# A list scheduler for a transformer kernel, with plain exponentials and the norms' small steps on GpSimd

## The chip, the core and the metric

The kernel runs on one core of one Trainium2 chip. The metric is the device time of one execution in microseconds. Lower is better. The engines are called PE (TensorE, matrix products and transposes), DVE (VectorE), ACT (ScalarE, activations and copies), POOL (GpSimd) and SP (SyncE, which issues most DMAs). All of them run at the same time, each through its own queue in a fixed order, and wait for one another through semaphores. SBUF is the on-chip memory; PSUM has eight banks of 128 x 512 floats, into which PE writes.

## What is computed

The input x has 32 batch elements of 128 tokens and 128 channels. A cross attention with 16 heads and a time bias comes first, then six layers of local attention and feed forward. In short:

```python
x = x + xattn(layernorm(x), ctx, ctx, deltas, mask)      # 16 heads, 4 key groups, head size 8
h = layernorm(x)
y = h
for i in range(6):
    y = attn(shift_tokens(y), Wqkv[i], q_scale[i], k_scale[i], Wo[i]) + y
    y = ffn(shift_tokens(y), ln_g[i], ln_b[i], W1[i], b1[i], W2[i], b2[i]) + y
x = x + y

def shift_tokens(t):     # second half of the channels comes from the token before
    a, s = split(t, 2, -1);  return concat([a, pad(s, one token)[:-1]], -1)

def attn(x, Wqkv, qs, ks, Wo):          # 16 heads of 64
    q, k, v = split(x @ Wqkv)
    q = rotary(l2norm(q) * qs);  k = rotary(l2norm(k) * ks)
    # windows of 32 tokens; each token sees the 32 tokens before it and itself
    return softmax(mask(8 * q @ k.T)) @ v @ Wo

def ffn(x, g, b, W1, b1, W2, b2):       # 341 hidden channels
    a, gate = split((layernorm(x) * g + b) @ W1 + b1)
    return (a * gelu(gate)) @ W2 + b2
```

## The kernel before

**Tiling.** A *unit* is one batch element in one layer: 128 tokens on the partitions. There are 6 x 32 = 192 units. Four batch elements form a *group* (GB = 4); each layer has eight groups, and the feed forward works on a whole group at once, 48 times in all. Matrix products with full precision are made of three products of parts (`split3`, lines 636 to 638).

**A unit.** PE makes four tiles of 128 x 512 queries and keys (`qk`, names pqk). ACT squares each (line 686), DVE sums the squares of each head (line 689) and multiplies the tile with two tables for the rotary embedding (line 694, two products t of 512 columns for each tile), POOL adds the two (line 700, result rt). Then comes the inverse norm of all 32 heads, `rsqrt_a`, `rsqrt_b`, `rsqrt_c`: a floor on DVE (line 118), a logarithm and an exponential on ACT (lines 126 and 128), and one Newton step in three small operations on DVE (lines 133, 135, 137). POOL multiplies the four rt tiles with it (line 723), PE transposes them (line 729), ACT copies the queries out (line 735) and the halves of the keys (lines 739 and 746; one half per unit goes to DVE, line 744). The values go through the output projection at once (`y`, names py), ACT copies them (line 762), and sixteen small DMAs on SP's queue lay each unit's rows out by windows (line 769, tiles ysh). The scores of half the heads lie in one PSUM bank (lines 781 and 786). DVE takes the row maxima (line 793). ACT makes the exponentials, eight pieces of 64 columns for each half, and each piece adds up its sum in an accumulator that a further instruction reads out (line 804). DVE inverts the sums (line 809), POOL scales the weights (line 813), DVE transposes them (line 817), and PE multiplies them with ysh (line 830, pO).

**A group.** Its input is transposed and shifted on PE: for each of the four elements, one transpose of half the channels and one product with a shift matrix for the others (lines 660 and 661, ax), written as two parts by ACT and DVE. After the four units come the residual (line 848), a DMA that shifts half of the channels by one token (line 851), the layer norm with the same `rsqrt` steps on 4 columns (line 116 and the shared lines), PE's products, three gelus on ACT (line 910) and the second product (line 935). After the third gelu, line 912 asks for one particular table of ACT's functions by name:

```python
            if i == 2:
                nc.scalar.preload_act_table_set("natural_log_exp_and_others")
```

The same call stands once in the prologue (line 140). ACT keeps one table of functions at a time; where an instruction needs a function that the table at hand lacks, the compiler puts a load (ACT_TABLE_LOAD) ahead of it.

**Order.** The order is written out by hand. `OFF`, `GOFF`, `OFF1` and `GOFF1` hold one place on a common scale for every operation of a unit, a group and the cross attention; `push` puts each operation into a heap by its time (a unit is given T = 13.3, a group four times that), and `drain` issues them in that order. Each engine's queue follows it. Buffers come from pools that rotate: five PSUM banks for products (pj), two for scores, one for the attention's result; eight rt, four yt, three kb.

**Weights.** The next layer's weights are loaded and split while the present layer runs (`prep_ops`), with places in the same scale.

Of the kernel before, what the change touches and what calls it, by code (L numbers as in the profile page):

```python
# [8 lines left out]
F32 = mybir.dt.float32  # L9
# [7 lines left out]
P = 128  # L17
# [5 lines left out]
NRT = 8  # L23
NYT = 4
NKB = 3
NQT = 3
EWD = (1,)
STORE = 0.4
MP1 = [23.0 + 1.2 * i for i in range(8)]
WV1, DH1, DL1 = [20.85, 22.05], 0.15, 0.3  # L30
PREP0, PREPT = 10.0, 7.0
SHIFT = 6.0
FFT = 7.0
MP = [31.47, 31.72, 31.97, 32.22, 32.47, 32.72, 32.97, 33.22]
WV, BIAS, DH, DL = [24.4, 25.4], 16.4, 0.06, 0.14
T1 = 7.0
NI1 = 180
OFF1 = dict(
    sc=[[0, 2, 26, 28], [32, 34, 73, 75], [93, 95, 139, 141], [154, 159, 170, 172]],
    mx=[[1, 3, 27, 29], [33, 35, 74, 76], [94, 96, 140, 142], [158, 164, 171, 173]],  # L40
    sb=[[4, 5, 30, 31], [36, 37, 77, 78], [97, 98, 143, 144], [165, 168, 174, 175]],
    ex=[[39, 41, 44, 48], [99, 100, 101, 102], [151, 152, 155, 160], [187, 189, 192, 196]],
    tp=[[42, 46, 51, 55], [126, 127, 128, 129], [153, 157, 163, 167], [190, 194, 199, 203]],
    st=[[45, 50, 54, 57], [130, 132, 134, 135], [156, 162, 178, 179], [193, 198, 202, 205]],
    pa=[[49, 53, 82, 83], [131, 133, 136, 137], [161, 166, 186, 188], [197, 201, 218, 220]],
    oT=[[84], [138], [191], [223]], pb=[[145], [146], [195], [227]], rl=[[147], [148], [200], [232]],
    at=[[149], [150], [204], [236]],
)
GOFF1 = dict(
    ldc=[-101], gst=[-121, -120], gr0=[-119], gr1=[-117, -116], gr2=[-115, -114, -113], xa=[-118], xb=[-112],  # L50
    px=[-89], pxe=[-88], pcx=[-100], pce=[-99], pk=[-77], ke=[-76], kd=[-75], pq=[-74, -73, -71, -67],
    qe=[-72, -69, -65, -62], qd=[-70, -66, -63, -60], pv=[-55], vt=[-11], td=[-110], ab=[-109, -108], ln=[-4],
    mkb=[-56], tbm=[-3], p2=[238], aT=[249], pw=[265], rs=[266], hst=[267, 268], hr0=[269], hr1=[292, 296],
    hr2=[299, 301, 302], xf1=[270], xf2=[303],
)
T = 13.3
NI = 331
OFF = dict(
# [28 lines left out]
def body(ctx: ExitStack, tc: tile.TileContext, x, ctx_in, fside, mask, xWq, xWk, xWv, xWo, xtw,  # L87
         Wqkv, q_scale, k_scale, Wo, ln_g, ln_b, W1, b1, W2, b2, cst, x1d, out):
    nc = tc.nc
    B = x.shape[0]  # L90
    L = Wqkv.shape[0]
    HID = W2.shape[1]
    NG = B // GB
    HC = [(0, 128), (128, 128), (256, HID - 256)]
    RT = HC[2][1]

# [939 lines left out]
```

## Time and profile before

| | us |
|---|---|
| median of 3 runs | 3326.27 |
| lowest and highest | 3325.03, 3327.11 |
| span of the profiled execution, first to last instruction | 3320.9 |
| PE busy in that span | 3155.8 |
| DVE busy | 2979.5 |
| ACT busy | 2834.9 |
| POOL busy | 2468.3 |
| 48 table loads ahead of a gelu (L910), 48 after (L912) | 61.6 each |

The profiled execution's own time is given only as its span. Busy time counts instructions at work; register, semaphore and DMA-issuing instructions are left out. In a row of instruction groups one reads the line of the source, the engine, the operation, the tile written and the tiles read with their shapes, how often, then busy time in us and the mean of one in ns, and last the engine's idle time just before them with what ended it. Instructions of one engine can overlap at their ends, so busy time divided by the count can be less than the mean of one.

### The profile page before, as it was taken

What the parts mean: (1) busy time and instruction counts of PE and PEld (TensorE: products, weight loads), DVE (VectorE), ACT (ScalarE), POOL (GpSimd) and SP (SyncE); (2) the same over time, 40 slices, a digit from 0 to 9 for tenths busy, and PEclk for the clock granted to TensorE, in tenths of its full rate; (3) what the DMA queues carried; (4) which work ended last, traced back from release to release, by engine and by line L of the source; (5) the groups of instructions that cost most, each with busy time, mean ns of one, the idle gap of its engine ahead of it and who ended that gap; (6) DMA issues with size and microseconds to landing.
All of it is one profiled execution on the core that took longest, in us unless ns stands there. A gap on an engine that the chain in (4) does not pass through costs nothing.

```text
span 3320.9 us, 102077 instructions
## 1 busy us (share of the span) xinstructions
PE 3155.8 (95%) x35979; PEld 2389.3 (72%) x35979; DVE 2979.5 (90%) x6954; ACT 2834.9 (85%) x9983; POOL 2468.3 (74%) x2284
## 2 busy tenths in 40 slices
PE   8999899999999999999999999999999999999997
PEld 5555677777777777777777777777777777777775
DVE  6666899999999999999999998998999998999995
ACT  6776888898888898889898889898888898898895
POOL 5655777777787777787787787786787776777873
PEclk9999999999999999999999999999999999999998
DMA  2110333332333332233332333332333332333332
GB/s 61 33 37 12 77 87 82 79 74 71 75 83 86 78 74 72 72 85 84 77 77 71 75 83 81 79 77 68 79 83 76 84 76 64 77 82 81 82 83 62
DMA packets 217966, 243.80 MB, mean 73 GB/s; under 512 B 83534, under 2 KB 112498, under 8 KB 217458
## 3 DMA queue, kind: packets, MB, share of 16 engines
q1 hardware_dynamic: 217026, 236.93, 28.8%
q8 instruction: 288, 4.72, 0.6%
q14 instruction: 220, 1.80, 0.2%
q10 hardware_dynamic: 432, 0.34, 0.0%
HBM read 25.31 MB, written 4.19 MB: 9 GB/s over the span
## 4 chain that ended last, share of the span: by engine, by line
PE 49%; DVE 32%; ACT 8%; issue 4%; DMA 3%; SPq 2%; POOL 1%; ACTq 0%; DVEq 0%; POOLq 0%
DVE t L694 10%; PE pO L830 8%; PE ptq L729 7%; DVE ss L689 6%; PE sc L786 4%; DVE rnv L118 3%; PE pa L542 3%; PE pqk L636 3%; PE pqk L638 3%; ACT pr L804 3%; PE pqk L637 3%; DVE mx L793 2%; DVE PT L817 2%; SPq L769 2%; PE py L636 2%
## 5 line engine op out<-in xcount | busy, mean ns | idle before, releaser
L700 POOL TENSOR_TENSOR rt<-t,t 128x512 f32<-128x512 f32 x768 | 980.3, 1286 | 372.8 <-DVE t L694 330.8
L694 DVE TENSOR_TENSOR t<-pqk,tab 128x512 f32<-128x512 f32 x1536 | 983.3, 681 | 115.9 <-ACT sq L686 110.3
L804 ACT ACTIVATE pr<-sc,mx 128x64 f32<-128x64 f32 x3072 | 915.7, 331 | 61.2 <-DVE PT L817 53.0
L723 POOL TENSOR_TENSOR rt<-rt,rny 128x512 f32<-128x512 f32 x768 | 777.4, 1043 | 214.1 <-DVE rny L137 213.4
L804 ACT ACTIVATION_READ_ACCUMULATOR pr<-sc,mx 128x1 f32 x3072 | 691.9, 225 | 0.0
L689 DVE TENSOR_REDUCE ss<-sq 128x8 f32<-128x512 f32 x768 | 517.4, 674 | 0.0
L830 PE MATMUL pO<-ysh,PT 128*32 128x128 f32 x10752 | 416.9, 275 | 53.3 <-DVE PT L817 48.7
L813 POOL TENSOR_TENSOR pr<-pr,rl 128x512 f32<-128x512 f32 x384 | 400.8, 1044 | 89.2 <-DVE rl L809 89.2
L686 ACT ACTIVATE sq<-pqk 128x512 f32<-128x512 f32 x768 | 429.3, 600 | 24.6 <-PE pqk L638 12.5
L830 PEld LDWEIGHTS pO<-ysh,PT 128*32 128x32 f32 x10752 | 367.1, 110 | 97.6 <-DVE PT L817 72.1
L762 ACT COPY yt<-py 128x512 f32<-128x512 f32 x768 | 416.8, 614 | 21.2 <-PE py L638 17.2
L729 PE MATMUL ptq<-cs,rt 128*128 128x128 f32 x3072 | 409.8, 278 | 22.2 <-DVE t L694 17.0
L729 PEld LDWEIGHTS ptq<-cs,rt 128*128 128x128 f32 x3072 | 334.5, 141 | 96.7 <-issue 52.5
L786 PE MATMUL sc<-kb,qT 128*32 128x128 f32 (+1 forms) x12288 | 375.1, 262 | 15.2 <-DVE kb L744 14.8
L786 PEld LDWEIGHTS sc<-kb,qT 128*32 128x32 f32 x12288 | 270.7, 109 | 114.5 <-issue 70.7
L636 PE MATMUL py<-mw,xsh 128*128 128x512 f32 x768 | 333.1, 434 | 8.9 <-ACT yt L762 5.8
L636 PE MATMUL pqk<-wqh,xsh 128*128 128x512 f32 x768 | 314.0, 409 | 4.8 <-ACT yt L762 2.8
L638 PE MATMUL py<-mw,xsl 128*128 128x512 f32 x768 | 301.9, 393 | 0.0
L638 PE MATMUL pqk<-wqh,xsl 128*128 128x512 f32 x768 | 300.9, 392 | 0.0
L637 PE MATMUL pqk<-wql,xsh 128*128 128x512 f32 x768 | 300.8, 392 | 0.0
L637 PE MATMUL py<-mw,xsh 128*128 128x512 f32 x768 | 300.6, 391 | 0.0
L735 ACT COPY qT<-ptq 128x512 f32<-128x512 f32 x384 | 208.1, 590 | 79.0 <-PE ptq L729 78.1
(168 smaller groups left out, 5756.8 us busy)
## 6 DMA issues: line engine op xcount, KB each, us to landing
ysh<-yt SPq DMA_DIRECT2D x3072, 64.0 KB
raw<-in_L_ffn_Wqkv SPq DMA_DIRECT2D x36, 256.0 KB
xsu<-xt SPq DMA_DIRECT2D x48, 127.0 KB
wor<-in_L_ffn_Wo SPq DMA_DIRECT2D x6, 512.0 KB
xt<-in_x SPq DMA_DIRECT2D x8, 256.0 KB
cx<-in_ctx SPq DMA_DIRECT2D x8, 256.0 KB
mk<-in_mask_BxS_ff SPq DMA_DIRECT2D x8, 256.0 KB
x_scratch<-xt SPq DMA_DIRECT2D x8, 256.0 KB
```

What stands on the lines that cost most here:

```text
L636: nc.tensor.matmul(pt, lh, rh, start=True, stop=False)
L637: nc.tensor.matmul(pt, lh, rl, start=False, stop=False)
L638: nc.tensor.matmul(pt, ll, rh, start=False, stop=True)
L686: nc.scalar.activation(V["sq", c], V["pp", c], AF.Square)
L689: nc.vector.tensor_reduce(V["ss"][:, c * 8:(c + 1) * 8], V["sq", c].rearrange("p (h d) -> p h d", d=64), axis=AX.X, op=ALU.add)
L694: nc.vector.tensor_tensor(V["t", k, c].rearrange("p h s d -> p h (s d)"), V["pp", c].rearrange("p (h d) -> p h d", d=64), w["tab"][:, c // ...
L700: nc.gpsimd.tensor_tensor(V["rt", c], V["t", 0, c], V["t", 1, c][:, :, ::-1, :], op=ALU.add)
L723: nc.gpsimd.tensor_tensor(rv, rv, V["rn"][:, c * 8:(c + 1) * 8].unsqueeze(2).to_broadcast([P, 8, 64]), op=ALU.mult)
L729: nc.tensor.transpose(V["ptq", c][:, k, :], V["rt", c][:, 2 * k:2 * k + 2].rearrange("p h s d -> p (h s d)"), ident)
L786: nc.tensor.matmul(sc[32 * c:32 * c + 32, :, wd, lo:64], qT[:, c, 32 * wd:32 * wd + 32], kT[:, c, :, 32 * wd - 32 + lo:32 * wd + 32], star ...
L804: nc.scalar.activation(pr[:, q, :], scv[:, q, :], AF.Exp, bias=mx[:, q:q + 1], accum_out=ls[:, q:q + 1])
L830: nc.tensor.matmul(pO[32 * wd:32 * wd + 32, j, :], PT[:, half, wd, blk, :], ysh[u][:, (2 * par + half) * P:(2 * par + half + 1) * P], star ...
```

## The change

The whole emission is rewritten. An operation is now recorded with its engine, two costs, a priority, and the buffers that it reads and writes (`S.op`). `Sched.run` then plays the engines in time: an engine that is free takes the first ready operation by priority (the unit's number plus a shift by name, `LATER`) whose buffers are to be had, and the order in which operations start is the order of issue. Costs are in a table by name (`COST`, an engine, the time that it is held, and the time to the result). Operations marked "E" or "G" need ACT's exponentials or gelus: a switch between the two adds 1.3 to the held time, and after a switch to "G" nothing marked "E" starts until three gelus have. Buffers are handed out by the scheduler: six PSUM banks for products, one for scores, one for the attention's result; ten rt, three yt, two kb, two t of 1024 columns.

In the operations themselves:

- The exponentials are eight plain activations for each half; one DVE operation adds up all eight sums (`sm`).
- The two table products of a tile are one DVE operation of 1024 columns (`tab`).
- The floor and the Newton step of every norm are five small operations on POOL (`newton`); logarithm and exponential stay on ACT.
- Both halves of the keys are copied by ACT (`evk`).
- A group's input tile has 192 columns: the channels, with the shifted half behind them. The shift is two DMAs, after the residual and after the feed forward (`shift`), and the shift products on PE are gone (`ax` is four transposes).
- The call that names ACT's table stands in the prologue only.

```diff
-        def tk(k, c):
-            V["t", k, c] = wk2.tile([P, 8, 2, 32], F32, tag=f"t{k}", name=f"t{k}")
-            nc.vector.tensor_tensor(V["t", k, c].rearrange("p h s d -> p h (s d)"),
-                                    V["pp", c].rearrange("p (h d) -> p h d", d=64),
-                                    w["tab"][:, c // 2, k, :].unsqueeze(1).to_broadcast([P, 8, 64]), op=ALU.mult)
+            S.op("tab", lambda: nc.vector.tensor_tensor(
+                t.t.rearrange("p (k h d) -> p k h d", k=2, d=64),
+                pp.t.rearrange("p (h d) -> p h d", d=64).unsqueeze(1).to_broadcast([P, 2, 8, 64]),
+                tab.t[:, c // 2].unsqueeze(2).to_broadcast([P, 2, 8, 64]), op=ALU.mult), pri, [pp, tab], [t])
...
-                nc.scalar.activation(pr[:, q, :], scv[:, q, :], AF.Exp, bias=mx[:, q:q + 1],
-                                     accum_out=ls[:, q:q + 1])
+                def ex(i):
+                    for k in range(4 * i, 4 * i + 4):
+                        nc.scalar.activation(pr.t[:, k * 64:(k + 1) * 64], sc.t[:, k * 64:(k + 1) * 64], AF.Exp,
+                                             bias=mx.t[:, k:k + 1])
+                for i in range(2):
+                    S.op("ex", lambda i=i: ex(i), pri, [sc, mx], [pr], table="E")
+                S.op("sm", lambda: nc.vector.tensor_reduce(sm.t, r8(pr), axis=AX.X, op=ALU.add), pri, [pr], [sm])
...
-        if eps is not None:
-            nc.vector.tensor_scalar(v, src, eps, None, op0=ALU.add)
-        else:
-            nc.vector.tensor_scalar(v, src, floor, None, op0=ALU.max)
...
-        if c == 0:
-            nc.vector.tensor_tensor(t, y, y, op=ALU.mult)
-        elif c == 1:
-            nc.vector.scalar_tensor_tensor(t, v, -0.5, t, op0=ALU.mult, op1=ALU.mult)
-        else:
-            nc.vector.scalar_tensor_tensor(y, t, 1.5, y, op0=ALU.add, op1=ALU.mult)
...
+    def newton(names, pri, V, src, n, floor, eps, pool_, cols):
+        v, y, t = [Buf(p) for p in pool_]
...
+        def f0():
+            if eps is not None:
+                nc.gpsimd.tensor_scalar(sl(v), cols(), eps, None, op0=ALU.add)
+            else:
+                nc.gpsimd.tensor_scalar(sl(v), cols(), floor, None, op0=ALU.max)
+
+        def f1():
+            nc.scalar.activation(sl(y), sl(v), AF.Ln)
+
+        def f2():
+            nc.scalar.activation(sl(y), sl(y), AF.Exp, scale=-0.5)
+
+        def f3():
+            nc.gpsimd.tensor_tensor(sl(t), sl(y), sl(y), op=ALU.mult)
+
+        def f4():
+            nc.gpsimd.tensor_tensor(sl(t), sl(t), sl(v), op=ALU.mult)
+
+        def f5():
+            nc.gpsimd.tensor_scalar(sl(t), sl(t), -0.5, 1.5, op0=ALU.mult, op1=ALU.add)
+
+        def f6():
+            nc.gpsimd.tensor_tensor(sl(y), sl(y), sl(t), op=ALU.mult)
+        S.op(names[0], f0, pri, [src], [v])
+        S.op(names[1], f1, pri, [v], [y], table="E")
+        S.op(names[2], f2, pri, [y], [y], table="E")
...
-            if i == 2:
-                nc.scalar.preload_act_table_set("natural_log_exp_and_others")
...
-                nc.tensor.transpose(G["ptx"][0:64, k, :], xb[:, 0:64], ident)
-                nc.tensor.matmul(G["ptx"][64:128, k, :], xb[:, 64:128], shift, start=True, stop=True)
...
+            nc.sync.dma_start(xt[g][1:113, :, 128:192], xt[g][0:112, :, 0:64])
+            nc.sync.dma_start(xt[g][113:P, :, 128:192], xt[g][112:P - 1, :, 0:64])
+        S.op("psh", f, pri, [X[g]], [XS[g]])
...
+                for o in cand[e]:
+                    if o.ready > t + 1e-9:
+                        continue
+                    if o.table and o.table != table and hold:
+                        continue
...
+                occ = o.occ
+                if o.table and o.table != table:
+                    table = o.table
+                    occ += 1.3
+                    if table == "G":
+                        hold = 3
+                if o.table == "G":
+                    hold -= 1
```

## The prediction

> **What bounds the kernel now.** I read the engines' shares first, then one steady stretch, then the instructions of that stretch.
>
> The page's first part and the head of its chain:
>
> ```profile
> PE 3155.8 (95%) x35979; PEld 2389.3 (72%) x35979; DVE 2979.5 (90%) x6954; ACT 2834.9 (85%) x9983; POOL 2468.3 (74%) x2284
> ...
> PE 49%; DVE 32%; ACT 8%; issue 4%; DMA 3%; SPq 2%; POOL 1%; ACTq 0%; DVEq 0%; POOLq 0%
> ```
>
> PE sets the end and DVE is close behind; ACT has only 15% to give. Busy time by stretch (columns: length, then PE, PEld, DVE, ACT, POOL, the granted clock, DMA share, GB/s):
>
> ```profile
> 200.00:300.00 100.00, 95.58 (x609) 56.30 (x609) 65.89 (x436) 68.50 (x141) 54.01 (x52) 1.00 0.05 14
> ...
> 1000.00:2000.00 1000.00, 964.16 (x11528) 747.19 (x11518) 935.22 (x1884) 885.28 (x3229) 771.98 (x709) 1.00 0.32 78
> ```
>
> The granted clock is full, so the work itself is the limit. The second stretch is inside the six layers. ACT's groups there give the unit of account:
>
> ```profile
> L804 ACT ACTIVATE pr<-sc,mx 128x64 f32<-128x64 f32 x1038 | 309.4, 331 | 19.7 <-DVE PT L817 17.1
> L804 ACT ACTIVATION_READ_ACCUMULATOR pr<-sc,mx 128x1 f32 x1038 | 233.9, 225 | 0.0
> L686 ACT ACTIVATE sq<-pqk 128x512 f32<-128x512 f32 x260 | 145.1, 600 | 6.3 <-PE pqk L638 2.5
> ...
> L746 ACT COPY kb<-ptq 64x512 f32<-64x512 f32 x65 | 37.8, 582 | 0.8
> L910 ACT ACT_TABLE_LOAD x16 | 20.5, 1283 | 0.3
> L912 ACT ACT_TABLE_LOAD x16 | 20.5, 1283 | 0.3
> ```
>
> A unit (one batch element in one layer) squares four times, so 260 squares are 65 units: one unit lasts 1000/65 = 15.38 us. Per unit PE is busy 964.16/65 = 14.83, DVE 14.39, ACT 13.62, POOL 11.88. There are 6 x 32 = 192 units, so 1 us per unit is 192 us of the kernel. Every change below is judged by which of these four becomes the largest.
>
> **The change, part by part, per unit.**
>
> **Exponentials (ACT).** All work on the tile pr took ACT 321.30 us in the stretch, for 1038/8 = 129.75 halves: 2.48 us a half. Without accumulators 8 plain pieces stay. None of 64 columns stands alone in this trace. The nearest row is four neighbours of 128 columns, also with a bias column per partition:
>
> ```profile
> 102.10 1.14 ACT L485 ACTIVATE kb<-pd,nct 128x128 f32<-128x128 f32 x4
> ```
>
> One lasts 0.373 (its group's mean), so the other three start (1.14 - 0.373)/3 = 0.256 apart. A 512-column copy starts about 0.49 after the one before it; from there to 0.256 is 0.234 for 384 columns, 0.61 ns a column, so 64 columns fewer is about 0.04 to 0.05: 0.21 a piece. Bounds: 0.13 (a 128x4 activation without a bias column starts so soon after another) and 0.256. At 0.21 a half is 7 x 0.21 + 0.33 = 1.80; the unit saves 2 x 0.68 = 1.36. With the bounds it saves 2.5 or 0.7.
>
> **Key copies (ACT, DVE).** One half copy per unit goes from DVE (L744, 0.695) to ACT, where its twin L746 takes 0.582: ACT +0.55, DVE -0.70.
>
> **Table loads (ACT).** This is the part that the diff hardly shows. The old line 912 loads the combined table by hand after each gelu; the new kernel has no such line outside the prologue. In the instruction order of the built program ACT then holds 534 table loads, against 97 before: 1 at the start, 48 ahead of a gelu, 230 ahead of a logarithm and 255 ahead of an exponential. The logarithm's loads name another table than the exponential's, so each norm flips twice. The logarithm and exponential of a norm stand one copy or square apart, with a load ahead of each. All 437 extra loads lie behind the first gelu: 437/192 = 2.28 per unit. The scheduler's table rule knows just two states, gelu and not gelu, so its order has no room for them. What one costs:
>
> ```profile
> 459.36 1.28 ACT L910 ACT_TABLE_LOAD   x1
> 460.65 1.83 ACT L910 ACTIVATE u<-pg,b1c 128x512 f32<-128x512 f32 x3
> 462.50 1.28 ACT L912 ACT_TABLE_LOAD   x1
> 463.80 1.08 ACT L735 COPY qT<-ptq 128x512 f32<-128x512 f32 x2
> ```
>
> From the gelus' end (462.48) to the next copy (463.80) is 1.32, and the overlap of about 0.1 that neighbours have (two copies in 1.08, 0.59 alone) is lost: 1.42. Bounds 1.28 and 1.42; I take 1.42: 2.28 x 1.42 = 3.24 us of ACT per unit. A load does not wait with the logarithm behind it, so it could use idle time of ACT; but the sum below leaves ACT none.
>
> Here the Trainium skill has a rule, and a harsher price. The page "ScalarE: Activation LUTs", section "Table sets: the hidden batching unit", says that one set holds both exp and ln and that mixing sets costs a load at each switch: the old order obeys, the new one does not. Its section "What ACT_TABLE_LOAD costs" gives 1283 ns plus a drain of 1380, 2.66 us a switch. The trace shows the 1283 to the digit, and 1.32 in all from end to start, no drain. By the rule the unit would pay 2.28 x 2.66 = 6.06, by the rows 3.24. I use the rows; the rule is a rival.
>
> ACT in sum: 13.62 - 1.36 + 0.55 + 3.24 = 16.05 us, above the present unit of 15.38.
>
> **Norm steps (DVE to POOL).** DVE loses 0.853 + 0.490 + 0.244 + 0.192 = 1.78 per unit for the queries' and keys' norm (L118, L133, L135, L137), and (0.733 + 0.212 + 0.925 + 0.417)/4 = 0.57 for the feed forward's. POOL gets five small operations for each. No such small one is in the trace. The line through
>
> ```profile
> L880 POOL TENSOR_TENSOR xn<-xn,fry 128x512 f32<-128x512 f32 x16 | 16.6, 1041 | 0.2
> ...
> L868 POOL TENSOR_TENSOR xn<-xsu,fmv 128x256 f32<-128x256 f32 x16 | 9.8, 616 | 0.0
> ```
>
> has 1.66 ns a column and 0.19 fixed: 0.24 for 32 columns, 0.20 for 4 (an estimate; bounds 0.12, the small clears of this trace, and 0.49, what DVE's L133 takes). POOL +5 x 0.24 + 5 x 0.20/4 = +1.45, to about 13.3. The first of the last four steps waits for the exponential; behind it in POOL's queue stand the multiplications by the norm and the additions that free the two t buffers, on which DVE's table products wait, and they hold PE's banks. In the new order POOL has a mean of 3.05 us of other work between its first step and that wait, but under 2.5 us in 88 of 192 units. The trip through ACT is two loads, two short activations and a copy: 2 x 1.42 + 2 x 0.27 + 0.5 = 3.9. So POOL stalls some 1.2 us per unit even if ACT comes at once: 14.5. That is below ACT's 16.05, but it passes ACT's lateness on.
>
> **Sums, table products (DVE).** Two sums a unit, one for each half, as L689 (0.674): +1.3. One 1024-wide product replaces two 512-wide ones: two take 1.28, so 0 to 0.15 each is saved; I take 0.08 x 4 = 0.3. DVE: 14.39 - 1.78 - 0.57 - 0.70 + 1.3 - 0.3 = 12.3.
>
> **Group input (PE).** Twelve narrow transposes and shift products go; from 1653.44 to 1655.79 they held PE for 2.35 us. Four plain transposes replace them, which start 0.42 before the next work (1643.39 to 1643.81): -1.9 per group, -0.48 per unit. PE: 14.35.
>
> **At nothing.** The shift now comes by DMA: 192 small DMAs instead of 48 on SP's queue. For the feed forward it was a DMA before; for the next layer's input there are seven other groups (seven times 61 us) to hide it. Behind a waiting shift stand the ysh transfers, which free the yt buffers (three instead of four); SP now waits 825.9 us in all for yt, so its queue has room. If that cover went, ACT's copies would wait; 0 to 0.2 us per unit. One score bank instead of two and two kb instead of three tie PE closer to ACT: a half's loop (scores 1.2, maximum 0.65, exponentials 1.8, hand-overs) is about 4 of every 8 us, hidden. The cross attention's work stays, and its norms come before the first gelu.
>
> **The sum.** Per unit: ACT 16.05, PE 14.35, POOL 13.3 with stalls 14.5, DVE 12.3. ACT becomes the bound. PE as the bound reached 14.83/15.38 = 96.4% busy. ACT's order was made without these loads, but the other engines have more slack than before, so I take 96%: 16.05/0.96 = 16.72. The unit grows by 1.34, 192 units by 257 us. The page gives the profiled execution as its span, 3320.9; the median of the runs is 5.4 above it, which I leave as it is: 3326.3 + 257 = 3583.
>
> **The rivals.**
>
> POOL's wait rules (20%): if ACT reaches the logarithm late by one burst of exponentials (1.8), the trip is 5.7 and POOL stalls about 2.7, to 16.0; two rings of equal length that wait for each other would run at perhaps 17.5: +2.1 x 192 = +400, 3730. For it: the queue's order. Against it: POOL's slack and ten rt buffers.
>
> The drain is real (4%): 18.9/0.96 = 19.7, +820, 4150. Against it: the rows above.
>
> Loads fall into idle time (10%): ACT pays 1.28 and the pieces cost less, 0.17: 13.62 - 1.9 + 0.55 + 2.92 = 15.2, at 97.5% 15.6: 3370 to 3450.
>
> Faster (4%): the exponentials' piece decides. At 0.13 it saves 2.5 and ACT, with loads of 1.28, needs 14.6; at 97.5% the unit is 15.0: -70, about 3255. The gain begins below 0.15 a piece, where ACT falls under 15.0. Against it: the row of 0.256, and the accumulator read itself starts 0.2 behind its piece.
>
> **How the numbers follow.** Likeliest (62%): 3583; between ACT 97.5% busy and 93% it gives 3533 to 3690. The range 3430 to 3760 leaves about 1 in 10 on each side: the last two rivals and the low edge of idle-time loads below, the drain and the upper part of POOL's case above. A difference under 0.2% (7 us) couldn't be told from none. Faster 0.04 is the last rival; same 0.02 lies between it and the idle-time loads; slower 0.94 is the rest.
>
> **What would show it.** In the changed profile: table loads of 1283 ns, 534 in number and some 685 us in sum; ACT the busiest engine in the layers, at 95% or more; PE near 86% of a unit of 16.7; POOL's wait for the exponential among the largest; the exponential's piece near 0.21 apart; DVE under 80%. It is wrong if ACT's busy share stays below 90% (then a wait rules), or if the loads overlap other ACT work.

## The result

The changed kernel takes 3763.83 us (median of four runs, 3758.95 to 3772.6) against 3325.65 for the kernel before: 1.1321 times as long, with a 95% interval of 1.1305 to 1.1337. That is 438 us more; 257 were forecast, and the time lies 4 us above the forecast's range. The profiled execution's span is 3757.1.

The first part of the page, and the stretches of the trace that answer to those shown of before (length; then PE, PEld, DVE, ACT, POOL busy; granted clock, DMA share, GB/s):

```profile
PE 3368.1 (90%) x35595; PEld 2335.1 (62%) x35595; DVE 2616.4 (70%) x5156; ACT 3225.6 (86%) x7540; POOL 2734.6 (73%) x3528
```

```profile
200.00:300.00 100.00, 91.42 (x529) 54.06 (x529) 55.95 (x367) 63.95 (x122) 49.44 (x60) 0.98 0.07 18
...
1000.00:2000.00 1000.00, 895.37 (x10009) 630.53 (x10008) 714.64 (x1146) 897.77 (x2112) 748.71 (x963) 0.97 0.30 69
```

No engine is full any more. In the layers PE and ACT are both at 90%, and the granted clock is 0.97 where it was 1.00. The unit of account is read most exactly from the residuals, 48 of four units each (the row gives, after the count, the shortest, median and longest of them in ns, and the start of the first and the last). First before, then after:

```profile
L848 DVE TENSOR_TENSOR xt<-pO,xt x48: 635/640/692, 402.2 to 3287.6; 128x512 f32<-128x512 f32 x48
```

```profile
L840 DVE TENSOR_TENSOR xt<-bank__68,xt x48: 674/680/692, 449.7 to 3729.9; 128x512 f32<-128x512 f32 x48
```

Between the first and the last lie 47 groups, 188 units: (3287.6 - 402.2)/188 = 15.35 us before and (3729.9 - 449.7)/188 = 17.45 after. The layers grow by 2.10 x 188 = 395 us, the head up to the first residual by 47, and the end is 6 shorter: 436 between the two spans. Busy time per unit is now PE 15.62, ACT 15.67, DVE 12.47, POOL 13.07 (the second stretch's numbers times 17.45/1000).

The table loads, in the groups of the page:

```profile
L374 ACT ACT_TABLE_LOAD x230 | 295.1, 1283 | 4.1
L377 ACT ACT_TABLE_LOAD x221 | 283.5, 1283 | 3.9
...
L873 ACT ACT_TABLE_LOAD x48 | 61.6, 1283 | 0.8
L812 ACT ACT_TABLE_LOAD x34 | 43.6, 1283 | 0.6
```

With the one at the start that is 534, and 685 us. ACT's queue around one norm, in the timeline (start, length):

```profile
1088.15 1.75 ACT L812 ACTIVATE pr__13818<-bank__67,mx__13883 128x64 f32<-128x64 f32 x8
...
1089.71 0.60 ACT L768 COPY kb__82<-bank__63 64x512 f32<-64x512 f32 x1
1090.33 0.58 ACT L769 COPY kb__82<-bank__63 64x512 f32<-64x512 f32 x1
1090.92 1.28 ACT L374 ACT_TABLE_LOAD   x1
1092.22 0.23 ACT L374 ACTIVATE ry__13953<-rv__13923 128x32 f32<-128x32 f32 x1
1092.47 0.59 ACT L765 COPY qT__13886<-bank__64 128x512 f32<-128x512 f32 x1
1093.08 1.28 ACT L377 ACT_TABLE_LOAD   x1
1094.37 0.23 ACT L377 ACTIVATE ry__13953<-ry__13953 128x32 f32<-128x32 f32 x1
```

Each load holds ACT for 1.30, from its start to that of the next instruction; the rows show no drain behind it. The eight exponentials of a half take 1.75.

### The profile page after: what moved, and what is told of

It reads as the page before. It is cut to its first block, busy times and chain, and to the rows that moved or that the text cites. A ratio compares the mean times of both kernels' runs of the same rounds, so it can differ in the third digit from the quotient of the medians.

```text
span 3757.1 us, 97639 instructions
## 1 busy us (share of the span) xinstructions
PE 3368.1 (90%) x35595; PEld 2335.1 (62%) x35595; DVE 2616.4 (70%) x5156; ACT 3225.6 (86%) x7540; POOL 2734.6 (73%) x3528
## 5 line engine op out<-in xcount | busy, mean ns | idle before, releaser
L374 ACT ACT_TABLE_LOAD x230 | 295.1, 1283 | 4.1
L377 ACT ACT_TABLE_LOAD x221 | 283.5, 1283 | 3.9
L797 PE MATMUL bank__67<-maskb,identb 128*128 128x512 bf16 x384 | 154.6, 403 | 97.3 <-ACT pr__18336 L812 2.2
L797 PEld LDWEIGHTS <-identb 128*128 128x128 bf16 x384 | 37.4, 97 | 90.9 <-issue 66.4
L873 ACT ACT_TABLE_LOAD x48 | 61.6, 1283 | 0.8
L812 ACT ACT_TABLE_LOAD x34 | 43.6, 1283 | 0.6
L840 DVE TENSOR_TENSOR xt<-bank__68,xt 128x512 f32<-128x512 f32 x48 | 32.6, 679 | 2.0 <-PE bank__68 L830 2.0
L768 ACT COPY kb__82<-bank__61 64x512 f32<-64x512 f32 x43 | 25.6, 596 | 0.7 <-PE bank__61 L407 0.7
L769 ACT COPY kb__82<-bank__61 64x512 f32<-64x512 f32 x43 | 25.0, 581 | 0.6
L769 ACT COPY kb__83<-bank__61 64x512 f32<-64x512 f32 x42 | 24.4, 581 | 0.8
L768 ACT COPY kb__83<-bank__61 64x512 f32<-64x512 f32 x42 | 24.9, 593 | 0.0
L896 DVE TENSOR_TENSOR xt<-bank__62,xt 128x512 f32<-128x512 f32 x12 | 8.2, 686 | 19.1 <-PE bank__62 L892 19.1
L768 ACT COPY kb__82<-bank__62 64x512 f32<-64x512 f32 x36 | 21.4, 595 | 0.1
L769 ACT COPY kb__82<-bank__62 64x512 f32<-64x512 f32 x36 | 20.9, 581 | 0.5
L768 ACT COPY kb__83<-bank__64 64x512 f32<-64x512 f32 x35 | 21.1, 603 | 0.0
L896 DVE TENSOR_TENSOR xt<-bank__61,xt 128x512 f32<-128x512 f32 x11 | 7.6, 688 | 19.1 <-PE bank__61 L892 19.1
L769 ACT COPY kb__83<-bank__64 64x512 f32<-64x512 f32 x35 | 20.4, 582 | 0.6
L769 ACT COPY kb__83<-bank__63 64x512 f32<-64x512 f32 x33 | 19.2, 582 | 0.6
L769 ACT COPY kb__82<-bank__66 64x512 f32<-64x512 f32 x33 | 19.2, 581 | 0.6
L768 ACT COPY kb__83<-bank__63 64x512 f32<-64x512 f32 x33 | 19.6, 595 | 0.0
L768 ACT COPY kb__82<-bank__66 64x512 f32<-64x512 f32 x33 | 19.6, 593 | 0.0
L769 ACT COPY kb__83<-bank__62 64x512 f32<-64x512 f32 x32 | 18.6, 581 | 0.5
```

Source lines behind the costliest of these rows:

```text
L374: nc.scalar.activation(sl(y), sl(v), AF.Ln)
L377: nc.scalar.activation(sl(y), sl(y), AF.Exp, scale=-0.5)
L768: S.op("evk", lambda: nc.scalar.copy(d.t[0:64, :, 0, :], p3()[0:64]), pri, [pt], [d])
L769: S.op("evk", lambda: nc.scalar.copy(d.t[64:128, :, 1, :], p3()[64:128]), pri, [pt], [d])
L797: nc.tensor.matmul(sc.t, identb, maskb, start=True, stop=True)
L812: nc.scalar.activation(pr.t[:, k * 64:(k + 1) * 64], sc.t[:, k * 64:(k + 1) * 64], AF.Exp, bias=mx.t[:, k:k + 1])
```

## The experiments

**Theories.** My theory after the result: the loads cost nearly all of the 438, more than ACT's own sum, because PE needs almost as much time per unit as ACT does and the order was planned without the loads. Rivals: POOL's wait for the norm's exponential sets the pace (the prediction's rival); another part of the rewrite costs time (accumulators, the norms' steps, the DMA shift, the order itself). Every kernel here computes the whole function.

### The loads alone

**e1_one_table.** The changed kernel with the old request for the common table after each third gelu; 97 loads instead of 534.

```diff
-            S.op("gel", lambda: nc.scalar.activation(...), pri, [pg, b1c], [u], table="G")
+            def gel():
+                nc.scalar.activation(...)
+                gelus[0] += 1
+                if gelus[0] % 3 == 0:
+                    nc.scalar.preload_act_table_set("natural_log_exp_and_others")
+            S.op("gel", gel, pri, [pg, b1c], [u], table="G")
```

> The changed kernel, with one line put back: after every third gelu ACT asks for the table that has both the logarithm and the exponential. 97 loads in place of 534, the order otherwise the same. If the loads are the whole loss: ACT falls from 15.7 to about 12.8 us a unit, PE is the bound again with 14.35, the unit comes to 14.9 to 15.3 and the kernel to 3240 to 3320, below the kernel before. If the list order itself (one score bank, small steps on POOL, fewer buffers) is the loss: above 3400.

**e2_told_of_flips.** All loads stay (530), but the scheduler is told of the flips: the logarithm gets a state of its own, so that each flip adds 1.3 to the planned time.

```diff
-        S.op(names[1], f1, pri, [v], [y], table="E")
+        S.op(names[1], f1, pri, [v], [y], table="L")
```

> The changed kernel, but the scheduler marks the norms' logarithms as a third table state, so that it plans 1.3 us for each flip; the program still has about as many loads (530). If ACT's sum alone sets the time (16.05 us a unit) and the misfit of the order is small: no change, 3740 to 3780. If the order that leaves no room for the loads costs the rest (17.45 against 16.05): ACT's idle time falls, the unit comes to 16.5 to 16.9, the kernel to 3560 to 3640.

**e3_late_norm.** All loads stay (509), and only the planned time until the norm's logarithm and exponential are done is 1.4 longer. So the list puts other work between them and POOL's step that waits.

```diff
-    ln=("ACT", .27, .24), ep=("ACT", .27, .24)
+    ln=("ACT", .27, 1.64), ep=("ACT", .27, 1.64)
...
-    lnf=("ACT", .22, .21), epf=("ACT", .22, .21)
+    lnf=("ACT", .22, 1.61), epf=("ACT", .22, 1.61)
```

> The changed kernel, but the scheduler is told that the results of a norm's logarithm and exponential come 1.4 us later, with ACT's held time unchanged; 509 loads. If POOL's wait for the norm (148 us in each 1000 of the layers) is what keeps PE and then ACT waiting: POOL does other work in that time, the wait shrinks, 3580 to 3660. If ACT's own queue is the trouble: 3730 to 3790.

**e4_before_flips.** The kernel before without the two lines that ask for the table: the old order by hand with 553 loads.

```diff
-            if i == 2:
-                nc.scalar.preload_act_table_set("natural_log_exp_and_others")
```

> The kernel before with the one line removed that asks for the common table after the gelus: 553 loads in place of 97, the order by hand unchanged. 456 more loads of 1.42 us are 3.37 us a unit: ACT 13.62 + 3.37 = 17.0. If ACT's sum sets the time at 96% busy: a unit of 17.7, 3770. If waits come on top as in the changed kernel (90% busy): 18.9, 4000. If the loads fell into ACT's idle time (1.76 us a unit): 3640 or less.

| | median us | ratio to before | us per unit |
|---|---|---|---|
| after | 3763.83 | 1.1321 (1.1305 to 1.1337) | 17.45 |
| e1_one_table | 3350.85 | 1.0086 (1.0062 to 1.011) | 15.27 |
| e2_told_of_flips | 3651.85 | 1.0998 (1.098 to 1.1017) | 16.79 |
| e3_late_norm | 3746.03 | 1.1274 (1.1257 to 1.1291) | 17.38 |
| e4_before_flips | 3717.75 | 1.1188 (1.1171 to 1.1205) | 17.44 |

Taking the loads away gives back 413 of the 438 us. That is 413/437 = 0.95 us of kernel time for each. But 3351 is above the 3240 to 3320 that were expected; where PE's saving went is a section of its own below. The stretch inside the layers, of e1 and then of e4:

```profile
1000.00:2000.00 1000.00, 986.59 (x11485) 709.75 (x11500) 818.46 (x1318) 831.65 (x2274) 861.25 (x1109) 1.00 0.34 80
```

```profile
1000.00:2000.00 1000.00, 853.44 (x10039) 664.30 (x10139) 811.21 (x1653) 949.09 (x2969) 678.42 (x623) 0.98 0.28 68
```

Without the loads PE is the bound, at 98.7% busy. With them in the old order ACT reaches 95%: 949.09 x 17.44/1000 = 16.55 of 17.44, with PE at 14.88. There 456 more loads cost 393 us, 0.86 each. So ACT can be kept nearly full in an order that wasn't planned for the loads, but there PE needs 1.7 us less per unit than ACT. In the changed kernel the two needs are 0.05 apart. The two kernels differ in more than that, so this comparison alone proves nothing.

e2 shows what planning is worth: with nearly as many loads the kernel is 112 us faster, and its unit of 16.79 is close to the forecast's 16.72. (The unit is read from an execution of 3633.81 us, 18 under the median.) e3 speaks against the rival. This is POOL's wait in the changed kernel (the bracket tells how long and for whom):

```profile
1094.68 0.24 POOL L380 TENSOR_TENSOR rw__14018<-ry__13953 128x32 f32<-128x32 f32 x1 [0.69 <-ACT ry__13953 L377]
```

Added up over the stretch from 1000 to 2000, POOL's idle time ahead of the norms' steps is 148 us after the change and 43 in e3. Of these 105 us per thousand, the kernel gained 18 us in all, 0.07 per unit, and e3 also has 25 loads fewer. The wait was real, and taking 71% of it away gained almost nothing.

### What one load costs, and when

**e14_load_at_norm.** e1 with one load of the common table ahead of each norm's logarithm: one load per norm, where the changed kernel has two.

```diff
         def f1():
+            if gelus[0]:
+                nc.scalar.preload_act_table_set("natural_log_exp_and_others")
             nc.scalar.activation(sl(y), sl(v), AF.Ln)
```

> e1 with one more load ahead of each norm's logarithm: 225 more loads, one a norm in place of two. ACT's sum is 12.76 + 1.17 x 1.42 = 14.4 us, under PE's 15.2. If loads cost only once ACT's sum passes PE's: 3351 to 3430. If each costs 0.9 us: 3555.

**e13_loads_elsewhere.** e1 with 384 loads that no norm waits for, right behind the eighth exponential of each half.

```diff
                     for k in range(4 * i, 4 * i + 4):
                         nc.scalar.activation(...)
+                    if i == 1:
+                        nc.scalar.preload_act_table_set("natural_log_exp_and_others")
```

> e1 with 384 more loads of the common table, two a unit, right behind the eighth exponential of each half; none stands in a norm. If a load costs by ACT's time in the queue, wherever it stands (0.9 to 0.95 us each, as in the changed kernel): 3351 + 355 = 3706. If it costs because it delays the norm that POOL waits for: 3500 or less.

**e9_half_flips.** e1 with the request after every sixth gelu (322 loads).

```diff
-                if gelus[0] % 3 == 0:
+                if gelus[0] % 6 == 0:
```

> e1, but the common table is asked for after every sixth gelu (every second group) alone: 322 loads, 225 more than e1. If the loads hurt by what they add to ACT's sum (12.76 + 225/192 x 1.42 = 14.4 us a unit, still under PE's 15.2): little, 3380 to 3450. If each load costs the kernel the same wherever ACT stands (413 us for 437 in the changed kernel): 3351 + 213 = 3564.

| | loads | median us | ratio to before | us per unit |
|---|---|---|---|---|
| e14_load_at_norm | 322 | 3455.55 | 1.0393 (1.0378 to 1.0409) | 15.85 |
| e13_loads_elsewhere | 481 | 3665.02 | 1.1023 (1.1002 to 1.1045) | 16.90 |
| e9_half_flips | 322 | 3552.87 | 1.0689 (1.0673 to 1.0705) | 16.34 |

The group of the added loads and the stretch in e14, then the stretch in e13:

```profile
L376 ACT ACT_TABLE_LOAD x225 | 288.7, 1283 | 3.9
```

```profile
1000.00:2000.00 1000.00, 959.43 (x11069) 684.61 (x11072) 789.06 (x1271) 901.02 (x2273) 831.88 (x1071) 1.00 0.33 77
```

```profile
1000.00:2000.00 1000.00, 922.58 (x10422) 648.45 (x10434) 744.09 (x1193) 910.39 (x2177) 780.97 (x1004) 1.00 0.31 73
```

The first load of a norm costs (3455.55 - 3350.85)/225 = 0.47 us, a third of the time that it holds ACT. From e14 to the changed kernel there are 212 more, and they cost (3763.83 - 3455.55)/212 = 1.45 each: the whole of a load and its lost overlap. I read the border between them as PE's need. In e14 ACT's sum, 901.02 x 15.85/1000 = 14.28, is still under e1's PE, 15.06; in the changed kernel, at 15.67, it is over it. Part of the 1.45 may be the lower granted clock (0.989 over the whole of e14, 0.965 in the changed kernel); no run takes that apart. e13's loads cost 314/384 = 0.82 each although no norm waits for them. That again takes the cause away from the norm's chain, and it fits ACT's sum: 910.39 x 16.90/1000 = 15.39. In e13 PE's need, 922.58 x 16.90/1000 = 15.59, is close to ACT's too; the clock in its stretch is 1.00, and still PE is busy for 92% only.

e9 was meant to show the same border and doesn't. Its 225 loads cost 202 us, 0.90 each, as if straight in proportion. But groups with all of the loads alternate with groups with none in it, so its mean says nothing of a border.

### The other parts of the change

These run on e1, so that the loads don't cover them.

**e7_accum.** The accumulators are back and the two DVE sums gone.

```diff
                         nc.scalar.activation(pr.t[:, k * 64:(k + 1) * 64], sc.t[:, k * 64:(k + 1) * 64], AF.Exp,
-                                             bias=mx.t[:, k:k + 1])
+                                             bias=mx.t[:, k:k + 1], accum_out=sm.t[:, k:k + 1])
...
-                S.op("sm", lambda: nc.vector.tensor_reduce(sm.t, r8(pr), axis=AX.X, op=ALU.add), pri, [pr], [sm])
```

> e1 with the exponentials' accumulators back and the sums on DVE gone (the scheduler's cost for the exponentials raised to 1.16). ACT has 1.4 us a unit more, DVE 1.3 less. If PE is the bound in e1 and the exponentials' saving lies off the path: 3340 to 3370. If ACT's relief is what brings e1 to 3351: 3420 or more.

**e8_newton_dve.** The norms' five small steps are back on DVE (the planned costs with them).

```diff
-            nc.gpsimd.tensor_tensor(sl(t), sl(y), sl(y), op=ALU.mult)
+            nc.vector.tensor_tensor(sl(t), sl(y), sl(y), op=ALU.mult)
```

> e1 with the norms' small steps on DVE as in the kernel before (the scheduler's costs as measured there). DVE goes from 12.5 to some 14.9 us a unit, POOL from 13 to 11.7. If PE alone is the bound: 3340 to 3380. If the move to POOL is worth something because DVE was close behind PE: 3400 to 3480.

| | median us | ratio to before | us per unit |
|---|---|---|---|
| e7_accum | 3370.86 | 1.0153 (1.0127 to 1.0179) | 15.38 |
| e8_newton_dve | 3451.91 | 1.0382 (1.0367 to 1.0398) | 15.85 |

The stretches of e7 and e8:

```profile
1000.00:2000.00 1000.00, 979.15 (x11404) 701.66 (x11406) 741.40 (x1180) 909.97 (x3289) 857.04 (x1100) 1.00 0.34 80
```

```profile
1000.00:2000.00 1000.00, 957.66 (x11070) 685.62 (x11089) 923.20 (x1667) 809.05 (x2196) 747.87 (x673) 1.00 0.32 77
```

With accumulators ACT has 909.97 x 15.38/1000 = 14.00 per unit instead of 12.70: the exponentials' saving is 1.3, as forecast. But where PE is the bound it is worth 20 us only. The steps on DVE bring DVE to 92% and cost 101 us: of the two parts tested here, the move to POOL gains more. The wide table products, the key copies and the smaller numbers of buffers were not tested alone.

### What PE does with its saving

Without the loads the kernel is still 27 us slower than before. The head makes that loss: e1's first residual starts at 447.3, 45 us later than before. The layers are 14 us shorter (15.27 for 15.35 a unit), but PE was to have 0.48 less per unit. Per unit PE is busy 14.80 before and 15.06 in e1 (986.59 x 15.27/1000). The timeline shows where it went. Before, then e1: products of three parts (start, length as modelled; the spacing of the starts is what counts).

```profile
1600.37 0.39 PE L636 MATMUL pqk<-wqh,xsh 128*128 128x512 f32 x1
1600.60 0.39 PE L637 MATMUL pqk<-wql,xsh 128*128 128x512 f32 x1
1600.83 0.39 PE L638 MATMUL pqk<-wqh,xsl 128*128 128x512 f32 x1
1601.06 0.39 PE L781 MATMUL sc<-maskb,identb 128*128 128x512 bf16 x1
```

```profile
1502.97 0.50 PE L402 MATMUL bank__62<-wch__18648,xh__20246 128*128 128x512 f32 x1
1503.31 0.40 PE L403 MATMUL bank__62<-wch__18649,xh__20246 128*128 128x512 f32 x1
1503.54 0.39 PE L404 MATMUL bank__62<-wch__18648,xl__20247 128*128 128x512 f32 x1
1503.87 0.65 PE L802 MATMUL bank__67<-kb__83,qT__21340 128*32 128x128 f32 x16
```

A tile in the midst of its kind holds PE for three times 0.23, to 0.24. In e1 the first product, here behind other work, has 0.34, and the last, ahead of other work, 0.33. On the mean over the stretch in e1 the first takes 0.330 behind other work and 0.238 behind its own kind. Of the tiles in the stretch, 157 of 618 begin behind other work before, and 387 of 621 in e1: the written order keeps a unit's products together, the list scheduler does not. A tile that no wait follows takes 0.726 on the mean before and 0.799 in e1. There are 1824 such tiles, 9.5 a unit: 0.69 us, of the 0.74 by which PE stands above the forecast (0.26 more instead of 0.48 less). I tried to prove it by reordering, and could not.

**e5_sticky, e6_sticky_flips.** PE takes a ready split product first if its last operation was one; on e1 and on the changed kernel.

```diff
+                seq = cand[e]
+                if e == "PE" and run[0]:
+                    seq = [o for o in seq if o.name in SPLIT] + [o for o in seq if o.name not in SPLIT]
-                for o in cand[e]:
+                for o in seq:
```

> The kernel with the common table put back after the gelus (e1, 3351), and one rule more in the scheduler: after a product in three parts PE takes another such product if one is ready. Tiles that begin behind other work fall from 1161 to 550 of 1824. If PE is the bound and pays about 0.15 us at each change of kind (0.095 on the first part, 0.055 on the last): 3.2 changes fewer a unit, 0.48 us, 3351 - 90 = 3260, faster than the kernel before. If the order is bound by something else, or the rule starves others: 3330 to 3400.

> The changed kernel with the same rule for PE and all its table loads (541). If only ACT's sum and its late norms set the 17.45 us of a unit: no change, 3740 to 3790. If PE, itself at 15.6 us a unit, and ACT at 15.7 hold each other up: PE needs some 0.5 us less, and a good part of it is seen, 3670 to 3720.

**e11_pairs.** Queries and keys, the value tiles, and the cross attention's scores each two tiles at a time, on e1. **e16_head_pairs.** Only the cross attention's scores in pairs. **e18_y_pairs.** e16 with the value tiles in pairs. The core of e16; the others are of the same form:

```diff
+            if h % 2 == 0:
+                two[:] = [(Buf("pj"), Buf("ysh")) for _ in range(2)]
+                pr2 = list(two)
+                def sc2():
+                    for i in range(2):
...
+                            nc.tensor.matmul(pr2[i][0].t[:, t * P:(t + 1) * P], qs[t].t[rows, tok],
+                                             kk.t[rows, tok], start=True, stop=True)
+                S.op("xsc2", sc2, pri, [kk, *qs], [a for a, _ in pr2], also=[b for _, b in pr2])
-            S.op("xsc", sc, pri, [kk, *qs], [ps], also=[sm])
```

> e1 with the scheduler's query, key and value tiles recorded two at a time, and the cross attention's scores two heads at a time; tiles that begin behind other work fall from 1161 to 834. If changes of kind are what PE lost: 1.7 fewer a unit at 0.15 us are 0.26 us, the unit falls from 15.27 to about 15.0, and the first residual comes some 10 to 25 us earlier than at 447: 3351 - 50 - 15 = 3286. If pairs hold too many banks and the order suffers, as with the rule in e5: 3370 or more.

> e1 with the cross attention's score products recorded two heads at a time, the layers as in e1. If single heads cost PE its overlap (63.1 us for these 512 products in the first 400 us, 38.0 before): the first residual comes 15 us earlier than 447, the layers' unit stays at 15.27, the kernel at 3335. If not: 3351 or more.

> e16 with the value tiles recorded two at a time; tiles that begin behind other work fall from 1160 to 1045. At 0.15 us a change: 0.6 a unit, 0.09 us, 3321 - 17 = 3304. If pairs of banks cost the order more than they save, as in e11: 3330 or more.

**e17_more_pe.** e16 with each group's four input transposes made five times: work that PE alone pays for (the planned cost with it).

```diff
+        def ax():
+            for _ in range(5):
+                tr4(pt.t, [xsg(g)[:, k] for k in range(GB)])
```

> e16 with the four transposes of each group's input made five times over (16 more of 0.11 us, 1.8 us for each of 48 groups; the scheduler's cost raised to match). If PE is the bound: 3321 + 85 = 3406. If something else holds the order: 3321 to 3350.

| | median us | ratio to before | us per unit |
|---|---|---|---|
| e5_sticky | 3535.22 | 1.063 (1.0606 to 1.0654) | 16.24 |
| e6_sticky_flips | 3979.93 | 1.1975 (1.1951 to 1.2) | 18.56 |
| e11_pairs | 3370.75 | 1.015 (1.0132 to 1.0168) | 15.47 |
| e16_head_pairs | 3321.13 | 0.9989 (0.998 to 0.9998) | 15.26 |
| e17_more_pe | 3408.11 | 1.0241 (1.0224 to 1.0258) | 15.72 |
| e18_y_pairs | 3375.85 | 1.0153 (1.0138 to 1.0168) | 15.58 |

The stretch of e5, and the residuals of e1 and of e16:

```profile
1000.00:2000.00 1000.00, 915.86 (x10687) 693.86 (x10703) 764.76 (x1218) 781.70 (x2106) 806.70 (x1035) 0.99 0.32 74
```

```profile
L841 DVE TENSOR_TENSOR xt<-bank__68,xt x48: 674/679/692, 447.3 to 3318.8; 128x512 f32<-128x512 f32 x48
```

```profile
L847 DVE TENSOR_TENSOR xt<-bank__68,xt x48: 673/680/692, 424.3 to 3292.9; 128x512 f32<-128x512 f32 x48
```

e5 halves the tiles that begin behind other work in the whole program (1161 to 550), and PE's busy time per unit does fall, from 15.06 to 915.86 x 16.24/1000 = 14.87. That is 0.19 of the 0.48 expected. Yet PE falls to 92% busy, and the kernel loses 184 us; I take it that the rule put back products for which other engines waited. e6 loses 216 us against the changed kernel, outside both of its expectations, and so decides nothing. e11 and e18 lose 20 and 55 us. So the price of a change of kind is seen in rows, and no run shows what a kernel gains without it. e17 shows that PE is the bound once the loads are gone: the four further passes are 48 x 1.8 = 86 us by the rows, and cost 87.

e16 settles the head. Its first residual starts at 424.3, where e1's starts at 447.3: 23 of the head's 45 us came from the cross attention's scores, issued one head at a time between other products. With its layers at 15.26 it is the best version: level with the kernel before to within 0.2%.

### The shift by DMA in the old order

**e10_before_dma_shift.** The kernel before with the group input of the change: two DMAs lay the shifted tile out, and PE makes four plain transposes of it. **e12_before_dma_shift2.** The DMAs are issued earlier (place -175 for -110). **e15_before_dma_split.** In e12 the second DMA of 127 rows is two, of 112 and 15.

```diff
+        def axd(_):
+            xs2 = G["xs2"] = wk2.tile([P, GB, P], F32, tag="xn", name="xs2", bufs=1)
+            nc.gpsimd.memset(xs2[0:1, :, 64:128], 0.0)
+            nc.sync.dma_start(xs2[:, :, 0:64], xg[:, :, 0:64])
+            nc.sync.dma_start(xs2[1:P, :, 64:128], xg[0:P - 1, :, 64:128])
...
-                nc.tensor.transpose(G["ptx"][0:64, k, :], xb[:, 0:64], ident)
-                nc.tensor.matmul(G["ptx"][64:128, k, :], xb[:, 64:128], shift, start=True, stop=True)
+                nc.tensor.transpose(G["ptx"][:, k, :], G["xs2"][:, k, :], ident)
```

> The kernel before with one part of the change alone: the group's input is shifted by two DMAs into a tile of its own, and PE makes four plain transposes of it in place of twelve narrow operations (its place in the order moved 2 us ahead). If PE's own work is the bound of the kernel before and this saves 1.9 us for each of 48 groups: 3326 - 91 = 3235 to 3260. If DVE, at 94% of a unit, takes over at once: 3290 to 3326. If the DMA comes late: above 3326.

> e10 with its two DMAs placed 10 us earlier in the order, away from the feed forward's own shift, behind which DVE waited up to 8 us in e10. If that neighbourhood was e10's loss and PE is the bound: 3235 to 3290. If DVE (94% busy) takes over: 3290 to 3326. If the shared buffer is the loss: above 3400.

> e12 with its shift in two DMAs, of 112 and 15 rows. If the 127-row DMA was what held SP's queue (the next issue took 7.05 us): the layers are free of it, and PE's 1.9 us a group show: 3235 to 3290. If DVE takes over as the bound: 3290 to 3326. If the shared buffer or the third DMA is the loss: above 3400.

| | median us | ratio to before |
|---|---|---|
| e10_before_dma_shift | 3686.6 | 1.1089 (1.1073 to 1.1106) |
| e12_before_dma_shift2 | 3680.53 | 1.1068 (1.1052 to 1.1085) |
| e15_before_dma_split | 3396.06 | 1.0215 (1.02 to 1.023) |

SP's queue in e12, then in e15 (start, length of the issue):

```profile
1033.47 0.68 SPq L659 DMA_DIRECT2D xs<-xt  x1
1034.20 0.74 SPq L660 DMA_DIRECT2D xs<-xt  x1
1034.98 7.05 SPq L174 DMA_DIRECT2D lgb<-in_L_ffn_ln_g  x1
```

```profile
1037.28 0.65 SPq L660 DMA_DIRECT2D xs<-xt  x1
1037.97 0.94 SPq L661 DMA_DIRECT2D xs<-xt  x1
1038.96 0.54 SPq L187 DMA_DIRECT2D w<-in_L_ffn_W  x1
```

I had expected a saving on PE, and e10 and e12 lose 10%: the issue behind the DMA of 127 rows takes 7.05 us, and the feed forward's own shift stands in the same queue (in e12 DVE waits for it 357.7 us in 47 waits). The split gives 284 us back. The kernel before has a DMA of 127 rows too, 48 times, and isn't held by it:

```profile
1019.40 0.76 SPq L851 DMA_DIRECT2D xsu<-xt  x1
1028.35 6.63 SPq L769 DMA_DIRECT2D ysh<-yt  x9
```

There the next issue comes 4.3 us or more behind the end of this one; at 4.3 it takes 2.72, and where it comes later still mostly under 0.7.

What stays in e15 is 71 us of loss, with PE at 91%: its saving was not to be had in the old order, whose places I did not plan anew. One candidate is in the trace: the feed forward's own shift is still one DMA of 127 rows, in the same queue as the three new ones, and DVE waits for it 77.0 us in 47 waits, where it waited 7.1 in 3 before. No run splits that one as well, so the cause is left open.

## Why the prediction was wrong, step by step

**Table loads: right.** 534 loads of 1283 ns and 685 us, as stated. The row-based price without a drain held: 1.30 from a load's start to the next instruction. The rival with the drain, built on the section "What ACT_TABLE_LOAD costs" of the Trainium skill's page "ScalarE: Activation LUTs", is out: it forecast 4150. That page's other rule, not to mix the sets, was the one that spoke against the change, and e1 puts 413 us on it.

**Exponentials: right.** (1.75 - 0.33)/7 = 0.203 apart, forecast 0.21; e7 confirms the saving of 1.3 on ACT.

**Norm steps, sums, table products: right.** The small POOL steps take 0.20 to 0.29; POOL has 13.07 per unit (forecast 13.3), DVE 12.47 (12.3) and 70%.

**ACT's sum: right.** 16.05 held 0.3 of lost overlap, which busy time doesn't count; 15.7 against 15.67 measured.

**PE 14.35 per unit: wrong.** It is busy 15.62 in the changed kernel and 15.06 in e1. The four transposes do take less (one set of four costs 87/(48 x 4) = 0.45 us in e17, where the twelve narrow ones took 2.35), but the sum took every other product at its old price, and by the rows the new order's changes between kinds of work took the saving. In the changed kernel a lower granted clock comes on top: the mean over the whole execution is 0.965, in e1 0.992. The last section has its rows: some 0.5 us a unit.

**"So I take 96%": the step that failed.** ACT was 89.8% busy; in the step's own terms its need of 16.05 filled not 96% of the unit but 16.05/17.45 = 92.0%. So 16.05/0.96 = 16.72 became 17.45: 0.73 x 192 = 140 of the 181 us missed. The reason that the step gave, more slack in the other engines, was false for PE: it was busy as long as ACT, and the order that wasn't planned for the loads had no slack there to take up their waits on each other. Of ACT's 91 us of waits between 1000 and 2000, 49 are copies and squares waiting for PE's products and 25 are waits for DVE; of PE's 103, 52 are waits for the transposed weights (PT), and 28 are waits until ACT's exponentials leave the one score bank. The prediction had that bank at nothing; e1, with the same bank and ACT in time, waits 3 us for it. This row shows one of PE's waits in the changed kernel, in which PT stands behind ACT's exponentials, POOL's scaling and DVE:

```profile
1090.85 0.30 PE L830 MATMUL bank__68<-ysh__13541,PT__13926 128*32 128x128 f32 x1 [1.39 <-DVE PT__13926 L820]
```

The missing plan is shown: e2 changes nothing else, its need fills 16.05/16.79 = 95.6%, and 112 us come back. The part of PE's lack of slack is argued. e4 (PE far below ACT, 95%), e14 (ACT below PE, 0.47 a load) and e13 (both needs near each other, 92%) agree with it, but each differs from the changed kernel in more than that. And PE's need is itself raised by the waits, through the clock: at e1's clock it would be nearer to 15.1 than to 15.62 (an estimate, from the last section). How the 140 us divide between the missing plan, the near needs and the clock isn't known beyond e2's 112, in which all three may have a share. The prediction's own sign, ACT under 90% with a wait that rules, came true at 89.8%. It is not one wait, though, but many small ones between two nearly full engines.

**"The cross attention's work stays": wrong by 47 us.** The work stays, its order doesn't. From 200 to 300 us PE makes 529 products where it made 609, at 91% busy and a clock of 0.98. e16 gives 23 of it back; the rest of the head was not taken apart.

**The rivals.** POOL's wait had 3730, the nearest number, by a cause that e3 excludes. The loads in idle time (3370 to 3450) were half true: one load per norm does cost only a third (e14, 3456), the second its full price. "Faster" needed a piece under 0.15.

## What to carry to other kernels

Ask for each engine's need after the change, and if two come out near each other in an order that wasn't planned for it, don't take for the fuller one the busy share of a planned order: here it was 90%, with the two 0.05 us apart. In the kernel before, planned by hand, PE reached 96% with DVE 0.4 us below it. A list scheduler that doesn't know a cost (the table flips) still pays it, and where the engines have nothing to spare the second load of a norm costs more than its own length, 1.45 for 1.28. Count what an engine pays for the order too: by the rows, PE's saving by fewer transposes was lost to changes between kinds of products, which no count of instructions shows.

## What was not expected of the hardware

A DMA over 127 rows held up its queue where the next issue came right behind it: that issue took 7.05 us, against 0.54 behind the one of 15 rows that followed one of 112, and the kernel 284 us more. The page "DMA: Bandwidth & Descriptors" of the Trainium skill, section "Why a DMA increments its semaphore by 16 and not by 1", says that the number of DMA engines at work is the largest up to 16 that divides the slowest dimension on both sides; 127 rows then leave one, 112 sixteen and 15 fifteen. These runs agree with it, but counted no engines. In the changed kernel the shifts are split so. Those whose landing the trace has land in 2.4 and 2.2 us:

```profile
xt<-xt SPq DMA_DIRECT2D x96, 112.0 KB, 2.4
...
xt<-xt SPq DMA_DIRECT2D x96, 15.0 KB, 2.2
```

The granted clock fell where PE had idle time: 0.99 in all kernels with PE at 96% or more of the layers, 0.965 in the changed kernel, 0.94 in e6, e10 and e12. But it isn't in proportion: e4, with PE at 85%, has 0.978. In short stretches of the changed kernel it is either 1.0 or 0.5. Here is one at 0.5, and then the second and third product of one tile inside it and of one behind it:

```profile
1019.00:1025.80 6.80, 5.11 (x43) 3.19 (x45) 6.13 (x11) 5.28 (x16) 6.11 (x8) 0.50 0.18 40
```

```profile
1024.27 0.63 PE L402 MATMUL bank__63<-wch__10737,xh__12571 128*128 128x512 f32 x1
1024.69 0.63 PE L403 MATMUL bank__63<-wch__10736,xl__12572 128*128 128x512 f32 x1
...
1026.53 0.39 PE L402 MATMUL bank__62<-wch__10978,xh__11604 128*128 128x512 f32 x1
1026.76 0.39 PE L403 MATMUL bank__62<-wch__10977,xl__11605 128*128 128x512 f32 x1
```

They start 0.42 apart at half the clock and 0.23 at the full one. Between its first and last residual the changed kernel has 53 such spells, 218 us together, with PE busy for 194 of them; e1 has one, of 17 us. At the full clock PE's work in them would take half of the 194, so some 0.5 us per unit (an estimate): most of the 0.56 by which PE is busier there than in e1. The spells follow waits of PE: of its 37 waits of over 2 us, 28 have one that begins within 9 us of the wait's start, of the 58 between 1.2 and 1.6 us only 12. So waits make PE slower as well as idle. What that costs the kernel, and what sets the clock beyond this, no run here tells.
